# LSH attention and a gated FFN on one core: five of a head's sixteen coefficient blocks from DMA transposes instead of comparisons

## The chip, the core and the metric

The kernel runs on one core of one Trainium2 chip. The metric is the device time of one execution in microseconds (us), the median of several runs. The profile comes from one further execution.

## What is computed

The input x is 16 batches (B) of 512 tokens (S) of 128 features. The attention has 16 heads (H) of 8 features. Each token gets one bucket per head, from the signs of six projections of its query, and the score of two tokens is multiplied by 63 if their buckets agree and by 62 if not. Cut to what matters:

```python
proj = jnp.einsum('bshe,en->bshn', qa, hyperplanes)
buckets = jnp.einsum('bshn,n->bsh', (proj >= 0).astype(jnp.int32), 2 ** jnp.arange(6))
scores = jnp.einsum('bhsd,bhtd->bhst', q, q) / jnp.sqrt(jnp.float32(E))
same = (b_hs[:, :, :, None] == b_hs[:, :, None, :]).astype(scores.dtype)
attn = jax.nn.softmax(scores * (NB - 2 + same), axis=-1)
out = jnp.einsum('bhst,bhtd->bhsd', attn, v)
```

Before and after the attention there are layer norms and a residual; then comes a feed-forward network (silu gate of two products, two gelu layers of 512 x 512, one product back to 128), again with layer norms and a residual. The matrix `same` of a head is symmetric: block (i, t) of 128 x 128 tokens is the transpose of block (t, i).

## The kernel before

One head j is 512 x 512 coefficients, in four row tiles t of 128 query tokens (NT = 4). The work of a head passes through the engines like this:

- **SP** (the sync engine's DMA queue, taken strictly in turn) gathers the head's operands: `ql` and `qr`, the query in three bf16 parts (lines 798 and 812), and `bb`, the head's 512 buckets in bf16, repeated on all 128 partitions (line 825).
- **PE** makes the scores `sp` of a row tile in a PSUM bank (line 847), one matmul each.
- **DVE** makes the coefficients `co` of a row tile (line 865): it compares the 512 buckets of `bb` with the bucket of the query token on each partition (`bj`, a pointer scalar) and adds 62. Then DVE multiplies `co` with `sp` into the f32 tile `l` and takes the maximum of each row in the same instruction (line 894).
- After two heads, a small DVE transpose (923), a DMA to memory (`md`, 928) and a DMA back that repeats the maxima over the partitions (`mb`, 940) bring the row maxima into the layout that is needed; **POOL** subtracts `mb` from `l` (947), **ACT** takes the exponential (952).
- When four heads are done, PE multiplies with the values (`av`, 973), which frees the four `l` buffers. Then follow the division, the residual and layer norm, and the feed-forward network of the batch (lines 1041 to 1188), which runs beside the heads of later batches.

The buckets of a batch are written to memory as `bkd` in rows: BR = 3 rows of BC = 172 values at a pitch of BP = 174. So `bb` has 522 columns, of which a comparison reads 3 x 172 = 516; `co` is one run of 516 per row tile, and the last four aren't used.

The order of all instructions is written down ahead of time by a small planner (class `Order`, lines 47 to 187). Every step is a process that asks for buffers, waits for events and offers an instruction to an engine with an estimated cost and a rank; the engine takes the offered instruction of the lowest rank (comparisons have 4, the logits of line 894 have 5, so a comparison that is ready goes first). Each engine then runs its list in that order. DMAs are modelled as one queue with a rate (DMA_RATE, KB per us, 160 before) and a landing time of 2.6 us. The planner's costs set the order only, not what an instruction takes on the chip.

Buffers around the change: 11 tiles `l` of 8 KB per partition (LB), four sets of `ql`, `qr` and `bb` (`row_bufs`), four `co` tiles of one row tile each (`co_bufs`), three PSUM banks for `sp`. A `co` buffer is given back after its own row tile's logits, and a set of rows after the head's last.

Of the kernel before, what the change touches and what calls it, by code (L numbers as in the profile page):

```python
# [21 lines left out]
P = 128  # L22
# [24 lines left out]
class Order:  # L47
# [7 lines left out]
    LAT = 0.3  # L55
    OWN = 0.2
    DMA_LAT = 2.6
    DMA_RATE = 160.0
    SWITCH = 4.0
    TABLE = 1.28  # L60

# [129 lines left out]
def tile_lsh_attention_ffn(  # L191
# [31 lines left out]
    DA = DH + 1  # L223
    NP = 3
    KS = NP * NP * DH
    BR, BC, BP = 3, 172, 174
    ROOT = float(np.float32(E**-0.5))
    GROUPS = (1, 2, 6, B)
    LATE = 20
# [2 lines left out]
    SCALE = 1.0 / math.sqrt(E)  # L232
    AHEAD = 1
    MH = 2
    LB = 11
    SLOTS = H * NT
    N = B * SLOTS

# [86 lines left out]
        mxpads.append(mp)  # L325
    bkts = []
    for i in range(2):
        bk = const.tile([H, BR, BP], BF16, name=f"bkt{i}")
        nc.vector.memset(bk, 0.0)
        bkts.append(bk)  # L330

# [6 lines left out]
    def dve(cost, rank, emit):  # L338
        return ("op", "DVE", cost, emit, rank, None)

    def act(cost, rank, emit, table=None):
        return ("op", "ACT", cost, emit, rank, table)
# [4 lines left out]
    def dma(kb, rank, emit, held=True, cost=0.35):  # L347
        return ("dma", "SP", cost, emit, rank, None, kb, held)

    def get(kind):  # L350
        return ("get", kind)
# [4 lines left out]
    def events(n):  # L356
        return [Event() for _ in range(n)]
# [4 lines left out]
    banks = Pool("b", 2)  # L362
    logit_bufs = Pool("l", LB)
    row_bufs = Pool("r", 4)
    co_bufs = Pool("co", 4)
    mx_bufs = Pool("mx", 2)
    mb_bufs = Pool("mb", 3)
    h_bufs = Pool("h", 3)
# [213 lines left out]
    def prep(b):  # L582
# [59 lines left out]
        def buckets():  # L642
            yield wait(read)
            kp = yield get(banks)
            pp = bank(kp, f"pp_{b}")
            yield pe(
                0.86,
                2,
                lambda: nc.tensor.matmul(
                    pp[0 : H * NH, :],  # L650
                    lhsT=hp_sb.rearrange("e h n -> e (h n)"),
                    rhs=qs,
                    start=True,
                    stop=True,
                ),
            )
            bits = p1.tile([H * NH, S], BF16, tag="bits", name=f"bits_{b}")
            yield dve(
                0.66,
                1,  # L660
                lambda: nc.vector.tensor_scalar(
                    bits, pp[0 : H * NH, :], hb_sb, 0.0, op0=ALU.add, op1=ALU.is_ge
                ),
            )
            od.put(banks, kp)
            kp = yield get(banks)
            bkp = bank(kp, f"bkp_{b}")
            yield pe(
                0.3,
                2,  # L670
                lambda: nc.tensor.matmul(bkp[0:H, :], lhsT=pw, rhs=bits, start=True, stop=True),
            )
            bk = bkts[b % 2]

            def evict():
                nc.scalar.copy(
                    bk[:, 0 : BR - 1, 0:BC],
                    bkp[0:H, 0 : (BR - 1) * BC].rearrange("h (r c) -> h r c", c=BC),
                )
                nc.scalar.copy(  # L680
                    bk[:, BR - 1, 0 : S - (BR - 1) * BC], bkp[0:H, (BR - 1) * BC : S]
                )

            yield act(0.53, -2, evict)
            od.put(banks, kp)
            bkd = dram.tile([H, BR * BP], BF16, tag="bkd", name=f"bkd_{b}")

            def write():
                yield dma(
                    16,  # L690
                    0,
                    lambda: nc.sync.dma_start(out=bkd, in_=bk.rearrange("h r c -> h (r c)")),
                )
                bkds[b] = bkd
                od.set(wrote)

            od.spawn(write())
            kp = yield get(banks)
            bjp = bank(kp, f"bjp_{b}")

            def columns():
                for t in range(NT):
                    nc.tensor.matmul(
                        bjp[:, ts(t, H)],
                        lhsT=bits[:, ts(t, P)],
                        rhs=pw,
                        start=True,
                        stop=True,
                    )

            yield pe(0.4, 2, columns)
            bj = p2.tile([P, NT * H], F32, tag="bj", name=f"bj_{b}")
            yield dve(0.13, 1, lambda: nc.vector.tensor_copy(bj, bjp[:, 0 : NT * H]))
            bjs[b] = bj
            od.put(banks, kp)
            od.set(columned)
# [70 lines left out]
    def gather(j, tag):  # L787
        b, h = divmod(j, H)
        yield wait(prepared[b])
        ql = p1.tile([KS, S], BF16, tag=f"ql{tag}", name=f"ql_{j}")  # L790
        qr = p1.tile([KS, S], BF16, tag=f"qr{tag}", name=f"qr_{j}")
        bb = p1.tile([P, BR * BP], BF16, tag=f"bb{tag}", name=f"bb_{j}")
        rows[j] = (ql, qr, bb, tag)

        yield dma(
            74,
            1 + j * 1e-3,
            lambda: nc.sync.dma_start(
                out=ql,
                in_=qds[b][1][h]  # L800
                .rearrange("i d s -> (i d) s")
                .unsqueeze(1)
                .to_broadcast([NP * DH, NP, S]),
            ),
            held=False,
            cost=0.75,
        )
        queue = nc.sync if j else nc.scalar
        yield dma(
            74,  # L810
            1 + j * 1e-3,
            lambda: queue.dma_start(
                out=qr,
                in_=qds[b][0][h]
                .rearrange("d j s -> (d j) s")
                .unsqueeze(0)
                .to_broadcast([NP, NP * DH, S]),
            ),
            held=False,
            cost=0.72 if j else 0.05,  # L820
        )
        yield dma(
            132,
            1 + j * 1e-3,
            lambda: nc.sync.dma_start(out=bb, in_=bkds[b][h].partition_broadcast(P)),
            cost=0.43,
        )
        od.set(gathered[j])
# [9 lines left out]
    def scores():  # L838
        for j in range(B * H):
            yield wait(gathered[j])  # L840
            ql, qr = rows[j][0:2]
            for t in range(NT):
# [9 lines left out]
                sps[j * NT + t] = (sp, k)  # L852
                od.set(scored[j * NT + t])

    def coeffs():
        for j in range(B * H):
            b, h = divmod(j, H)
            yield wait(gathered[j])
            bb = rows[j][2]
            for t in range(NT):  # L860
                k = yield get(co_bufs)
                co = p1.tile([P, BR * BC], BF16, tag=k, name=f"co_{j}_{t}")

                def emit(c=t * H + h, bb=bb, co=co, b=b):
                    nc.vector.tensor_scalar(  # L865
                        co,
                        bb.rearrange("p (r c) -> p r c", c=BP)[:, :, 0:BC],
                        bjs[b][:, c : c + 1],
                        float(NBKT - 2),
                        op0=ALU.is_equal,  # L870
                        op1=ALU.add,
                    )

                yield dve(0.39, 4, emit)
                cos[j * NT + t] = (co, k)
                od.set(weighed[j * NT + t])
                od.loose()

    def logits():
        for j in range(B * H):  # L880
            kl = yield get(logit_bufs)
            if j < SINGLES or j % MH == 0:
                km, pair = (yield get(mx_bufs)), []
                mx = mxpads[int(km[2:])]
            l = p1.tile([P, NT, S], F32, tag=kl, name=f"l_{j}")
            base = len(pair) * NT
            for t in range(NT):
                i = j * NT + t
                yield wait(scored[i])
                yield wait(weighed[i])  # L890
                (sp, ks), (co, kc) = sps.pop(i), cos.pop(i)

                def emit(t=t + base, sp=sp, co=co, l=l[:, t, :], mx=mx):
                    nc.vector.tensor_tensor_reduce(  # L894
                        out=l,
                        in0=co[:, 0:S],
                        in1=sp,
                        scale=1.0,
                        scalar=-3.0e38,
                        op0=ALU.mult,  # L900
                        op1=ALU.max,
                        accum_out=mx[:, t : t + 1],
                    )

                yield dve(0.61, 5, emit)
                od.put(score_banks, ks)
                od.put(co_bufs, kc)
                if t < NT - 1:
                    od.loose()
            od.put(row_bufs, rows.pop(j)[3])  # L910
            ls[j] = (l, kl)
            pair.append((j, l))
            if j < SINGLES or len(pair) == MH:
                od.spawn(maxima(pair, mx, km))
            if j % GH == GH - 1:
                od.spawn(attend(j // GH))
            od.loose()
# [403 lines left out]
```

## Time and profile before

| what | value |
|---|---|
| median of 3 runs | 1372.26 us (1371.28 to 1372.66) |
| the profiled execution, its own time | 1373.08 us |
| the profiled execution, its span | 1371.3 us |
| mean granted TensorE clock | 0.991 |
| busy over the span: PE, DVE, ACT, POOL | 96%, 90%, 82%, 89% |
| DMA: moved, mean rate | 175.39 MB, 128 GB/s |
| L865 comparison, 1024 times | 455.0 us busy, 472 ns each |
| L894 logits, 1024 times | 665.7 us busy, 681 ns each |
| L947 subtraction on POOL, 256 times | 1156.1 us busy, 4552 ns each |

How to read it: "busy" counts the time in which an engine has at least one instruction under way; the records of PE overlap each other, so a busy PE isn't one at its limit. A line such as "L865 DVE TENSOR_SCALAR co<-bb,bj" is the group of instructions that line 865 of the kernel issues on DVE, writing `co` from `bb` and `bj`; after the bar stand its busy time in us, the mean of one in ns, and how long the engine had been idle before these instructions and what ended that idle time. The DMAs that SP issues are shown with the time SP takes to issue them, not the time until the data lands.

### The profile page before, as it was taken

To read this page: it belongs to the slowest core of one execution; us is meant where nothing else is said; L and a number is where in the kernel's file an instruction comes from. 1 tells how busy PE (TensorE), PEld (TensorE's weight loads), DVE (VectorE), ACT (ScalarE), POOL (GpSimd) and SP (SyncE) were. 2 spreads that over 40 slices of the span, in tenths; PEclk is the share of its full clock that TensorE was granted. 3 is DMA by queue.
4 is the path that set the end of the run, shared out by engine and by line. 5 is a ranking of instruction groups with operands and counts; after the bars stand their busy time and mean duration, and the time that the engine had idled before them with its cause. 6 is when DMAs were issued, how large, how long until landed. Compare 5 with 4: busy or idle time off the path is not lost.

```text
span 1371.3 us, 21177 instructions
## 1 busy us (share of the span) xinstructions
PE 1317.3 (96%) x5922; PEld 550.9 (40%) x5922; DVE 1236.0 (90%) x3989; ACT 1127.8 (82%) x1607; POOL 1217.1 (89%) x319
## 2 busy tenths in 40 slices
PE   9999999999889999999999999999999999999996
PEld 3433334334334434343434434343434434343443
DVE  5999999999889999999999999999999999998210
ACT  2567798999779888988989888988989888988852
POOL 1599999999999999999999999999999999999400
PEclk9999999999899999999999999999999999999998
DMA  5756455445435455445545455454545454453000
GB/s 143 194 148 157 133 150 145 140 140 141 134 106 153 125 130 142 138 138 132 147 116 147 129 134 135 139 139 135 142 124 141 135 134 135 132 122 101 24 8 8
DMA packets 159837, 175.39 MB, mean 128 GB/s; under 512 B 34280, under 2 KB 117480, under 8 KB 159720
## 3 DMA queue, kind: packets, MB, share of 16 engines
q1 hardware_dynamic: 156909, 170.56, 45.4%
q10 hardware_dynamic: 2811, 3.48, 0.8%
q8 instruction: 47, 0.77, 0.2%
q14 instruction: 70, 0.57, 0.1%
HBM read 154.81 MB, written 19.17 MB: 127 GB/s over the span
## 4 chain that ended last, share of the span: by engine, by line
PE 50%; DVE 24%; POOL 9%; issue 8%; DMA 6%; ACT 2%; SPq 1%; POOLq 0%; DVEq 0%; ACTq 0%
PE hp L1122 18%; PE av L973 12%; DVE l L894 11%; PE sp L847 9%; DVE co L865 8%; POOL l L947 8%; PE w L1088 4%; PE yp L1156 3%; DMA mb<-md 3%; DMA bb<-bkd 1%; DMA qd<-q 1%; PE op L994 1%; PE vp L760 1%; POOL rs_x L561 1%; DMA qr<-qd 1%
## 5 line engine op out<-in xcount | busy, mean ns | idle before, releaser
L947 POOL TENSOR_TENSOR l<-l,mb 128x2048 f32<-128x2048 f32 x256 | 1156.1, 4552 | 43.4 <-DVE mxpad L894 24.0
L894 DVE CUSTOM_DVE_ANT_0 l<-co,sp 128x512 f32<-128x512 bf16 x1024 | 665.7, 681 | 13.8 <-PE av L973 6.9
L952 ACT ACTIVATE l<-l 128x2048 f32<-128x2048 f32 x256 | 484.6, 1907 | 40.9 <-POOL l L947 39.4
L1122 PE MATMUL hp<-h,h 128*128 128x512 f32 x1024 | 498.6, 596 | 0.3 <-ACT h L1135 0.3
L865 DVE TENSOR_SCALAR co<-bb,bj 128x516 bf16<-128x516 bf16 x1024 | 455.0, 472 | 3.3 <-DMA bb<-bkd 3.1
L847 PE MATMUL sp<-qr,ql 72*128 72x512 bf16 x1024 | 358.0, 382 | 26.7 <-DVE mxpad L894 22.5
L1122 PEld LDWEIGHTS hp<-h,h 128*128 128x128 f32 x1024 | 190.1, 190 | 185.6 <-issue 151.6
L973 PE MATMUL av<-l,vaug 128*32 128x512 f32 x2048 | 263.6, 603 | 0.0
L847 PEld LDWEIGHTS <-ql 72*128 72x128 bf16 x1024 | 94.1, 97 | 313.9 <-issue 290.7
L1088 PE MATMUL w<-xnt_f,w 128*128 128x512 f32 x256 | 132.0, 601 | 2.5 <-ACT a L1074 2.4
L952 ACT ACT_TABLE_LOAD x86 | 110.3, 1283 | 1.5
L1251 PE MATMUL activity<-still 128*128 128x512 bf16 x402 | 106.6, 385 | 1.0 <-DVE still L280 1.0
L973 PEld LDWEIGHTS av<-l,vaug 128*32 128x32 f32 x2048 | 47.4, 109 | 116.5 <-issue 93.9
L894 DVE DVE_READ_ACCUMULATOR2_ANT mxpad<- 128x1 f32 x1024 | 85.7, 84 | 0.0
L450 POOL TENSOR_TENSOR rs_y<-ve_y,mhalf 128x4 f32<-128x4 f32 x16 | 16.1, 1006 | 67.1 <-issue 34.7
L1057 DVE TENSOR_TENSOR h<-w,a 128x512 f32<-128x512 f32 x64 | 43.7, 682 | 35.2 <-PE w L1088 30.3
L1135 ACT ACT_TABLE_LOAD x58 | 74.4, 1283 | 0.9
L987 ACT COPY avs<-av 128x512 f32<-128x512 f32 x64 | 37.0, 578 | 40.0 <-PE av L973 39.9
L1088 PEld LDWEIGHTS w<-xnt_f,w 128*128 128x128 f32 x256 | 46.9, 191 | 53.1 <-issue 21.8
L1156 PEld LDWEIGHTS yp<-w,h 128*128 128x128 f32 x512 | 65.0, 196 | 7.3 <-issue 4.0
L1156 PE MATMUL yp<-w,h 128*128 128x128 f32 x512 | 66.6, 281 | 0.1
L1251 PEld LDWEIGHTS <-still 128*128 128x128 bf16 x402 | 39.1, 99 | 56.5 <-issue 19.0
(94 smaller groups left out, 941.7 us busy)
## 6 DMA issues: line engine op xcount, KB each, us to landing
mb<-md SPq DMA_DIRECT2D x256, 256.0 KB
bb<-bkd SPq DMA_DIRECT2D x256, 130.5 KB
ql<-qd SPq DMA_DIRECT2D x256, 72.0 KB
qr<-qd SPq DMA_DIRECT2D x255, 72.0 KB
qd<-q SPq DMA_DIRECT2D x96, 128.0 KB
xta<-in_L_attn_x_dram SPq DMA_DIRECT2D x16, 256.0 KB
xtr<-in_L_attn_x_dram SPq DMA_DIRECT2D x16, 256.0 KB
out_dram<-y SPq DMA_DIRECT2D x16, 256.0 KB
```

The source lines that it names most:

```text
L847: nc.tensor.matmul(sp, lhsT=ql[:, ts(t, P)], rhs=qr, start=True, stop=True)
L865: nc.vector.tensor_scalar(co, bb.rearrange("p (r c) -> p r c", c=BP)[:, :, 0:BC], bjs[b][:, c : c + 1], float(NBKT - 2), op0=ALU.is_equal, ...
L894: nc.vector.tensor_tensor_reduce(out=l, in0=co[:, 0:S], in1=sp, scale=1.0, scalar=-3.0e38, op0=ALU.mult, op1=ALU.max, accum_out=mx[:, t : ...
L947: lambda: nc.gpsimd.tensor_tensor(l, l, mb.unsqueeze(1).to_broadcast([P, NT, S]), op=ALU.subtract),
L952: yield act(1.82, 0, lambda: nc.scalar.activation(l, l, AF.Exp, scale=SCALE), "exp")
L973: nc.tensor.matmul(av[k * Q : (k + 1) * Q, :], lhsT=va[:, t, c : c + Q], rhs=ls[gg * GH + k][0][:, t, :], start=(t == 0), stop=(t == NT - 1),)
L1057: lambda: nc.vector.tensor_tensor(h[:, c, :], g2, a, op=ALU.mult),
L1088: lambda: nc.tensor.matmul(gp, lhsT=w_sb[which][:, 0, ts(c, P)], rhs=xnt, start=True, stop=True),
L1122: lambda i=i: nc.tensor.matmul(hp, lhsT=w[:, i, ts(c, P)], rhs=hin[:, i, :], start=(i == 0), stop=(i == NC - 1),),
L1135: nc.scalar.activation(h[:, c, :], hp, AF.Gelu, scale=sc[:, c : c + 1])
L1156: nc.tensor.matmul(yp[:, ts(t, E)], lhsT=h[:, i, ts(t, P)], rhs=w_sb["w3"][:, i, :], start=(i == 0), stop=(i == NC - 1),)
L1251: nc.tensor.matmul(bk, lhsT=still, rhs=still.unsqueeze(1).to_broadcast([P, NT, P]), start=start, stop=stop,)
```

## The change

Row tiles 0 and 1 make part of the coefficients of the later row tiles (TURNED = 2). Row tile 0 is compared in full, 4 blocks of 128 columns. Row tile 1 is compared in its blocks 1 to 3 only, row tiles 2 and 3 in blocks 2 and 3 only. The missing five blocks (1,0), (2,0), (3,0), (2,1) and (3,1) come from two DMA transposes per head, which SP issues: one turns the blocks 1 to 3 of row tile 0, the other the blocks 2 and 3 of row tile 1. The logits of row tile t wait for the transposes that write into it (none for 0, one for 1, two for 2 and 3).

For this, `co` becomes one tile of a whole head (4 x 512 bf16, 4 KB per partition), with three buffers, given back after the head's last logits. The buckets are kept in 4 rows of 128 at a pitch of 130, so that a comparison reads 4, 3, 2 or 2 rows of 128 columns. The `l` buffers go from 11 to 10. The planner is told a DMA rate of 240, a cost of 0.6 us for a transpose on SP, and new costs of the comparisons.

```diff
-    DMA_RATE = 160.0
+    DMA_RATE = 240.0
...
-    BR, BC, BP = 3, 172, 174
+    BP = P + 2
+    TURNED = 2
...
-    LB = 11
+    LB = 10
...
-    co_bufs = Pool("co", 4)
+    co_bufs = Pool("co", 3)
...
+    turns = [events(TURNED) for _ in range(B * H)]
+
+    def turn(j, co, i):
+        yield dma(
+            2 * 32 * (NT - 1 - i),
+            0.5,
+            lambda: nc.sync.dma_start_transpose(
+                out=co[:, i + 1 :, ts(i, P)], in_=co[:, i, (i + 1) * P :]
+            ),
+            cost=0.6,
+        )
+        od.set(turns[j][i])
+
     def coeffs():
...
-            bb = rows[j][2]
+            bb = rows[j][2].rearrange("p (r c) -> p r c", c=BP)
+            k = yield get(co_bufs)
+            co = p1.tile([P, NT, S], BF16, tag=k, name=f"co_{j}")
+            cos[j] = (co, k)
             for t in range(NT):
-                k = yield get(co_bufs)
-                co = p1.tile([P, BR * BC], BF16, tag=k, name=f"co_{j}_{t}")
-
-                def emit(c=t * H + h, bb=bb, co=co, b=b):
+                r = min(t, TURNED)
+
+                def emit():
+                    c = t * H + h
                     nc.vector.tensor_scalar(
-                        co,
-                        bb.rearrange("p (r c) -> p r c", c=BP)[:, :, 0:BC],
+                        co[:, t, r * P :].rearrange("p (r c) -> p r c", c=P),
+                        bb[:, r:, 0:P],
                         bjs[b][:, c : c + 1],
                         float(NBKT - 2),
                         op0=ALU.is_equal,
                         op1=ALU.add,
                     )
 
-                yield dve(0.39, 4, emit)
-                cos[j * NT + t] = (co, k)
+                yield dve(0.08 + 0.09 * (NT - r), 4, emit)
                 od.set(weighed[j * NT + t])
-                od.loose()
+                if t < TURNED:
+                    od.spawn(turn(j, co, t))
+            od.loose()
...
                 yield wait(weighed[i])
-                (sp, ks), (co, kc) = sps.pop(i), cos.pop(i)
+                for e in turns[j][:t]:
+                    yield wait(e)
+                sp, ks = sps.pop(i)
+                co = cos[j][0][:, t, :]
...
-                        in0=co[:, 0:S],
+                        in0=co,
...
-                od.put(co_bufs, kc)
                 if t < NT - 1:
                     od.loose()
+            od.put(co_bufs, cos.pop(j)[1])
             od.put(row_bufs, rows.pop(j)[3])
```

The eviction of the buckets on ACT becomes one copy in place of two, and the `bkt`, `bkd` and `bb` tiles take the new shape.

More of the change, by code (lines that the diff above doesn't have):

```diff
@@ L327, in tile_lsh_attention_ffn @@
     for i in range(2):
-        bk = const.tile([H, BR, BP], BF16, name=f"bkt{i}")
+        bk = const.tile([H, NT, BP], BF16, name=f"bkt{i}")
         nc.vector.memset(bk, 0.0)
@@ L676, in evict @@
                 nc.scalar.copy(
-                    bk[:, 0 : BR - 1, 0:BC],
-                    bkp[0:H, 0 : (BR - 1) * BC].rearrange("h (r c) -> h r c", c=BC),
-                )
[L680 to L684, printed above, removed]
+                    bk[:, :, 0:P], bkp[0:H, :].rearrange("h (r c) -> h r c", c=P)
+                )
+            yield act(0.5, -2, evict)
             od.put(banks, kp)
-            bkd = dram.tile([H, BR * BP], BF16, tag="bkd", name=f"bkd_{b}")
+            bkd = dram.tile([H, NT * BP], BF16, tag="bkd", name=f"bkd_{b}")
             def write():
@@ L791, in gather @@
         qr = p1.tile([KS, S], BF16, tag=f"qr{tag}", name=f"qr_{j}")
-        bb = p1.tile([P, BR * BP], BF16, tag=f"bb{tag}", name=f"bb_{j}")
+        bb = p1.tile([P, NT * BP], BF16, tag=f"bb{tag}", name=f"bb_{j}")
         rows[j] = (ql, qr, bb, tag)
```

## The prediction

> **What bounds the kernel now.** I read the table of stretches first, because shares over the whole span mix start, steady part and tail. Columns: length, then busy time (and instructions) of PE, PE weight loads, DVE, ACT and POOL, then granted clock, DMA share and GB/s.
>
> ```profile
> 754.20:831.30 77.10, 74.97 (x342) 31.75 (x342) 76.61 (x250) 67.40 (x86) 74.72 (x20) 1.00 0.49 136
> 831.30:908.40 77.10, 76.14 (x350) 31.55 (x348) 76.52 (x246) 69.50 (x88) 76.09 (x20) 1.00 0.50 136
> ```
>
> The chain of work repeats every two batches (the same yp step at 596, 750 and 904 us), so a batch of 16 heads takes 77.1 us, a head 4.82 us. The span of 1371.3 us is 256 x 4.82 = 1234 us and 137 us of start and tail. In a steady batch DVE is busy 76.5 us (99%), POOL 74.7 to 76.1 us. Three engines are full together; a cheaper one hands the end to the next.
>
> Second, the groups of instructions by shape, for the prices:
>
> ```profile
> L947 POOL TENSOR_TENSOR l<-l,mb 128x2048 f32<-128x2048 f32 x256 | 1156.1, 4552 | 43.4 <-DVE mxpad L894 24.0 <-DMA mb<-md 14.1 <-ACT junk L407 3.1
> ...
> L894 DVE CUSTOM_DVE_ANT_0 l<-co,sp 128x512 f32<-128x512 bf16 x1024 | 665.7, 681 | 13.8 <-PE av L973 6.9 <-PE sp L847 5.1
> L865 DVE TENSOR_SCALAR co<-bb,bj 128x516 bf16<-128x516 bf16 x1024 | 455.0, 472 | 3.3 <-DMA bb<-bkd 3.1
> ...
> L661 DVE TENSOR_SCALAR bits<-pp,hb_sb 96x512 bf16<-96x512 f32 x16 | 11.8, 737 | 0.0
> ...
> L455 DVE TENSOR_SCALAR nm_f<-mv_f,rs_f 128x1 f32<-128x1 f32 x64 | 9.2, 208 | 3.8 <-POOL rs_f L450 3.8
> ```
>
> DVE almost never waits. POOL needs 16 x 4.552 + 3 x 1.006 = 75.9 us per batch, 98% of the period. PE's busy time overlaps itself; by starts (0.43 us for an f32 record of hp or w, 0.215 sp, 1.85 per 16 av) its batch needs about 73 us.
>
> Third, SP, whose instructions are not counted as busy: its own waits (total us, times, longest) and its timeline.
>
> ```profile
> SPq L928 <- DVE co L865: 227.2, 104, 6.0
> SPq L798 <- PE sp L847: 134.4, 146, 3.3
> ...
> SPq L940 <- POOL l L947: 46.7, 50, 5.0
> ```
> ```profile
> 718.00 0.55 SPq L928 DMA_DIRECT2D md<-mt  x1
> 718.60 0.72 SPq L812 DMA_DIRECT2D qr<-qd  x1
> 719.38 0.43 SPq L825 DMA_DIRECT2D bb<-bkd  x1
> 720.37 0.77 SPq L798 DMA_DIRECT2D ql<-qd  x1
> 721.25 0.45 SPq L940 DMA_DIRECT2D mb<-md  x1
> ```
>
> SP takes its DMAs strictly in turn. A head needs ql 0.78 + qr 0.72 + bb 0.41 + mb 0.40 + half of md 0.56 = 2.59 us, its share of the batch's twelve others (qd, xta, xtr, out, bkd, at 0.33 to 0.6) about 0.28, and some 0.08 us between neighbours (718.60 to 719.38 for a 0.72), about 0.35: 3.2 of 4.82 us. So 1.6 us per head are free, and SP already stands behind DVE for long stretches.
>
> **The change, part by part.** *Comparisons (L865).* L661 and L455 give a TENSOR_SCALAR's fixed time: 737 - 512/0.96 = 204 ns, and 208 for one element. L865 then is 204 + 516/(2 x 0.96) = 473 ns, as measured: two elements per cycle. A head had 4 x 516 = 2064 elements and keeps 512 + 384 + 256 + 256 = 1408. At the same rate that takes 656/1.92 = 342 ns off 4.82 us of DVE, 87 us over the span.
>
> *The form of the comparison, a rule against the change.* Source rows go from 3 of 172 to 4, 3, 2 and 2 of 128. The row before: 2 elements per cycle.[...] By the row the comparisons cost 16 x 0.342 = 5.5 us less per batch[...]. At worst one comparison stops DVE for nearly a whole POOL instruction each head, with only one l (0.6 us) done beside it: 4.6 + 4.1 - 0.7 = 8.0 us, 2185 us. I keep the row's rate for the likeliest case, and the rule as a rival.
>
> *Transposes on SP.* Added: two per head, 512 in all. No row shows one. Nearest rows for issuing: md 0.56, ql 0.78 (the longest, with the most row pieces). At 0.56 with gaps, 1.3 us fit in the free 1.6; at 0.78, 1.7 us, SP needs 4.9 us per head and is full. A full queue that also waits on DVE and POOL in turn cannot run at 100%; at 95% that is 5.16 us per head. Not below nothing: issuing is added work. I take 0.78 at 95%: 256 x (5.16 - 4.82) = +87 us, less nothing for DVE, which is no longer last.
>
> *Transposes on the DMA engines.* 5 x 32 KB = 160 KB per head beside 175.39 MB / 256 = 685 KB. As plain traffic the share goes from 0.49 to 0.60: hidden.[...] No row decides; I take little extra[...].
>
> *The new waits.* Each transpose waits on SP for its comparison; behind it stand md and mb, for which POOL waits, and the gathers. On DVE, l of t = 1 waits for one transpose and t = 2, 3 for two, with all DVE work behind. md to the mb that reads it takes 2.8 us in the timeline (709.44 to 712.28), the nearest row for a landing. With three co buffers of a whole head, comparisons may lead by one to two heads, 4.8 to 9.6 us: cost nothing, if that lead is real; without it up to 2.8 us per head. I take nothing, since SP's lateness is already counted.
>
> *Eleven to ten l buffers.* DVE waited for av to free l 6 times, 6.9 us in all: between nothing and one such wait (up to 2.3 us) in each of 64 groups, 147 us; I take 5 us. The reason it can't gain: a buffer less adds only waits.
>
> *The rest at nothing:* one ACT copy in place of two (0.43 + 0.28 to about 0.57 us, 16 times, ACT is 88% busy), 520 for 522 columns of bb. The planner's rate of 240 moves emission order, not work.
>
> **Sum.** 1371.3 + 87 + 5 = 1463 on the profiled span; its own execution is 1373.1, 1.8 longer than its span, and the median 1372.3 lies 0.8 under that. About 40 heads of the start and the end run while SP has room; there DVE's 0.34 us per head is a gain, 13 us off: **1450 us**.
>
> **Rivals.**
> - *Shared ports*[...]: 1570 to 2185 us, middle near 1800. For: the row counts become even, POOL is busy 97% of the time[...]. Against:[...] the instruction's encoded shape is not in the profile.
> - *It works, on the other side:* transposes land inside the lead, issue near md's 0.56, and DVE falls to 4.43 us per head. Then POOL's 75.9 us per batch ends last: at most 1.2 x 16 = 20 us. It still waits for ve and mb now and then (2 us per batch now), so I give two thirds: 1358 us, 1352 to 1369. It decides as long as a transpose's issue stays under 0.7 us (SP's free 1.6 us halved, less the gap). For: DVE is at 99%. Against: POOL at 98% and PE at 95% leave little.
> - *Nothing to see:* same as that, with the lost l buffer eating it: 1370 to 1375.
>
> **Chances.** SP or DMA queue full 0.36[...]; shared ports 0.33; works 0.25; nothing to see 0.06. A difference under 0.2% can't be told from none here. Faster 0.25, same 0.06, slower 0.69. The range from 1352 to 1850 leaves out the upper half of the shared-port case (0.17) and a sliver below.[...]
>
> **What would show it.** DVE busy down by 80 to 90 us with TENSOR_SCALAR near 471, 404 and 337 ns: the comparison step. Records of 337, 304 and 271 ns, gaps on DVE or POOL of 1 to 4 us beside them, or POOL instructions well over 4.55 us: shared ports. SP issue of a transpose near 0.8 us, SP without gaps, and POOL waiting for mb: my likeliest.[...] POOL over 99% in steady batches: the gain. I am wrong if the issue is near 0.5 us[...].

## The result, and the profile after

| | before | after |
|---|---|---|
| median | 1371.77 us (4 runs) | 2171.43 us (2154.74 to 2192.97, 4 runs) |
| ratio | | 1.579, 95% interval 1.568 to 1.590 |
| span of the profiled execution | 1371.3 us | 2177.5 us |

The ratio leaves out the execution of 2192.97 us, which ran at a lower granted clock (0.820) than the other three (0.831 to 0.834).

The change makes the kernel 58% slower. The forecast was 1450 us, and the time lies outside its range too (1352 to 1850). A head now takes (2177.5 - 137)/256 = 7.97 us in place of 4.82: close to the 8.0 us, 2185 us, that the prediction had priced for the worst case of a rival, "shared ports".

From the page after, its head and the chain of work that ended last:

```profile
span 2177.5 us, 22144 instructions
## 1 busy us (share of the span) xinstructions
PE 1575.4 (72%) x5901; PEld 627.8 (29%) x5901; DVE 1881.4 (86%) x3989; ACT 1135.4 (52%) x1593; POOL 1217.1 (56%) x319
...
DVE 48%; PE 25%; issue 15%; DMA 8%; SPq 3%; ACT 1%; POOL 0%; DVEq 0%; POOLq 0%; ACTq 0%
```

POOL works exactly as long as before (1217.1 us) in a span 806 us longer; it is now idle 44% of the time. DVE, which was to get lighter by 87 us, is busy 645 us longer. The groups of DVE by shape say where:

```profile
L880 DVE TENSOR_SCALAR co<-bb,bj 128x256 bf16<-128x256 bf16 x512 | 713.2, 1400 | 0.0
L913 DVE CUSTOM_DVE_ANT_0 l<-co,sp 128x512 f32<-128x512 bf16 x1024 | 677.6, 676 | 101.3 <-PE sp L844 47.9 <-PE av L992 42.1 <-DMA co<-co 9.2
L880 DVE TENSOR_SCALAR co<-bb,bj 128x512 bf16<-128x512 bf16 x256 | 297.5, 1162 | 48.8 <-DMA bb<-bkd 48.6
L880 DVE TENSOR_SCALAR co<-bb,bj 128x384 bf16<-128x384 bf16 x256 | 102.6, 401 | 0.0
```

The comparison of 256 columns takes 1400 ns on average, that of 384 columns 401 ns. The longer one is faster. Its source has three rows, that of the others four or two. 401 ns is near 204 + 384/1.92 = 404, the old rate: 1.92 columns per ns, about twice what the rows L661 and L455 of the kernel before show, (737 - 208)/511 = 1.04 ns a column. The logits (676 ns) are as before. DVE waits for a transpose's landing only 9.2 us in all.

The same tile's view, with minimum, median and maximum in ns, shows that the mean hides two kinds of record, and what SP pays for a transpose:

```profile
L880 DVE TENSOR_SCALAR co<-bb,bj x1024: 239/352/4685, 26.4 to 2070.5; 128x512 bf16<-128x512 bf16 x86, 128x256 bf16<-128x256 bf16 x85
...
L860 SPq DMA_TRANSPOSE co<-co x512: 1167/1205/2642, 27.5 to 2074.6; - x171
```

A comparison can be as short as 239 ns and as long as 4685 ns, a little over one POOL instruction (4528 ns). By the trace, 235 of the 768 comparisons with four or two rows take over 0.6 us, and every one of them ends within 0.08 to 0.16 us after a POOL instruction has ended. None of the other 533 lies wholly inside a subtraction of POOL (L966). Of the 256 with three rows the longest takes 418 ns; 55 of them lie wholly inside a subtraction, at 401 ns in the mean.

Who waits on SP, and POOL's wait for the maxima (us in total, times, longest):

```profile
SPq L860 <- DVE co L880: 430.7, 165, 9.6
```
```profile
POOL l L966 <- DMA mb<-md: 544.0, 92, 29.0
```

SP takes its DMAs in turn: by the trace, none of its 1846 issues here begins before the one ahead of it has ended. It isn't full in this kernel: from 900 to 1000 us its issues take 65% of the time and the short gaps between them, some 0.09 us each, 6%; for the rest it waits, most of all for comparisons. POOL's wait for `mb`, which the prediction named as a sign of a full SP, stands here beside an SP with room.

### The profile page after: what moved, and what is told of

Same layout as the page of the kernel before. It is cut to its first block, busy times and chain, and to the rows that moved or that the text cites. A ratio compares the mean times of both kernels' runs of the same rounds, so it can differ in the third digit from the quotient of the medians.

```text
span 2177.5 us, 22144 instructions
## 1 busy us (share of the span) xinstructions
PE 1575.4 (72%) x5901; PEld 627.8 (29%) x5901; DVE 1881.4 (86%) x3989; ACT 1135.4 (52%) x1593; POOL 1217.1 (56%) x319
## 4 chain that ended last, share of the span: by engine, by line
DVE 48%; PE 25%; issue 15%; DMA 8%; SPq 3%; ACT 1%; POOL 0%; DVEq 0%; POOLq 0%; ACTq 0%
DVE co L880 30%; DVE l L913 14%; PE hp L1141 8%; PE av L992 6%; PE sp L844 6%; DMA bb<-bkd 4%; DMA co<-co 2%; PE w L1107 2%; DVE h L1076 1%; PE activity L1270 1%; SPq L860 1%; DMA ql<-qd 1%; PE yp L1175 1%; DVE mxpad L913 1%; PE op L1013 1%
## 5 line engine op out<-in xcount | busy, mean ns | idle before, releaser
L966 POOL TENSOR_TENSOR l<-l,mb 128x2048 f32<-128x2048 f32 x256 | 1154.8, 4528 | 738.4 <-DMA mb<-md 544.0
L880 DVE TENSOR_SCALAR co<-bb,bj 128x256 bf16<-128x256 bf16 (+2 forms) x1024 | 1101.9, 1091 | 48.8 <-DMA bb<-bkd 48.6
L844 PE MATMUL sp<-qr,ql 72*128 72x512 bf16 x1024 | 429.3, 444 | 560.0 <-DVE mxpad L913 554.8
L913 DVE CUSTOM_DVE_ANT_0 l<-co,sp 128x512 f32<-128x512 bf16 x1024 | 677.6, 676 | 101.3 <-PE sp L844 47.9
L1141 PE MATMUL hp<-h,h 128*128 128x512 f32 x1024 | 577.2, 675 | 0.0
L1141 PEld LDWEIGHTS hp<-h,h 128*128 128x128 f32 x1024 | 216.9, 216 | 435.4 <-issue 411.1
L992 PE MATMUL av<-l,vaug 128*32 128x512 f32 x2048 | 297.8, 685 | 2.1 <-DVE y L1199 2.1
L844 PEld LDWEIGHTS <-ql 72*128 72x128 bf16 x1024 | 105.6, 107 | 488.5 <-issue 461.6
L1107 PE MATMUL w<-xnt_f,w 128*128 128x512 f32 x256 | 158.8, 721 | 7.9 <-DVE h L1076 7.2
L1154 ACT ACTIVATE h<-hp,h2s 128x512 f32<-128x512 f32 x64 | 41.8, 685 | 53.9 <-PE hp L1141 53.5
L474 ACT ACTIVATE yb<-o,nm_o,rs_o 128x128 f32<-128x128 f32 x64 | 29.5, 461 | 74.9 <-DVE nm_o L456 65.7
```

Source lines behind the costliest of these rows:

```text
L844: nc.tensor.matmul(sp, lhsT=ql[:, ts(t, P)], rhs=qr, start=True, stop=True)
L880: nc.vector.tensor_scalar(co[:, t, r * P :].rearrange("p (r c) -> p r c", c=P), bb[:, r:, 0:P], bjs[b][:, c : c + 1], float(NBKT - 2), op0 ...
L913: nc.vector.tensor_tensor_reduce(out=l, in0=co, in1=sp, scale=1.0, scalar=-3.0e38, op0=ALU.mult, op1=ALU.max, accum_out=mx[:, t : t + 1],)
L966: lambda: nc.gpsimd.tensor_tensor(l, l, mb.unsqueeze(1).to_broadcast([P, NT, S]), op=ALU.subtract),
L992: nc.tensor.matmul(av[k * Q : (k + 1) * Q, :], lhsT=va[:, t, c : c + Q], rhs=ls[gg * GH + k][0][:, t, :], start=(t == 0), stop=(t == NT - 1),)
L1107: lambda: nc.tensor.matmul(gp, lhsT=w_sb[which][:, 0, ts(c, P)], rhs=xnt, start=True, stop=True),
```

## The experiments

The theory after the result, "shared ports": a comparison with an even number of source rows (here four or two) can't run while POOL's subtraction runs. The name stands for a reason that no run here shows; the runs show the wait alone. Rivals: "SP and DMA" (the transposes' issue or traffic sets the pace), "late transposes" (DVE waits for their landing), and the tenth `l` buffer.

**Even rows alone, on the kernel before.** No transposes, eleven `l` buffers.

```diff
-    BR, BC, BP = 3, 172, 174
+    BR, BC, BP = 4, 128, 130
```

> The kernel before with one edit: the buckets in four rows of 128 (pitch 130) in place of three of 172. No transposes, eleven l buffers. Theory 'shared ports'[...]: comparison records with a minimum near 337 ns, a mean over 1000 ns, longest near 4.7 us; DVE per head 4.82 - 1.89 + 1.00 = 3.9 us, plus POOL's 4.6, less 0.7 done beside it: 7.8 us per head, 137 + 256 x 7.8 = about 2130 us. Rival 'SP and DMA' (the 1.2 us that SP spends on each transpose set the pace): 1372 us within 5. Rival 'late transposes' (DVE waits for their landing): 1372 us.

Measured: 2259.68 us, ratio 1.647 (1.644 to 1.651). One line of shapes, with no transpose in the kernel, makes it slower than the whole change does. The comparisons (minimum, median and maximum), then one stretch of the timeline (start, length, engine, instruction):

```profile
L865 DVE TENSOR_SCALAR co<-bb,bj x1024: 300/345/4714, 26.2 to 2143.7; 128x512 bf16<-128x512 bf16 x171
```
```profile
998.94 18.10 POOL L947 TENSOR_TENSOR l<-l,mb 128x2048 f32<-128x2048 f32 x4
...
999.86 3.76 DVE L865 TENSOR_SCALAR co<-bb,bj 128x512 bf16<-128x512 bf16 x1
...
1005.24 7.43 DVE L865 TENSOR_SCALAR co<-bb,bj 128x512 bf16<-128x512 bf16 x2
...
1013.80 3.39 DVE L865 TENSOR_SCALAR co<-bb,bj 128x512 bf16<-128x512 bf16 x1
```

POOL's four instructions follow each other at 4.525 us, so they end at 1003.46, 1007.99, 1012.51 and 1017.04. DVE's comparisons end at 1003.62, 1012.67 (the second of two) and 1017.19: each time 0.15 us after a POOL instruction ends, wherever it began. In the whole trace 250 comparisons take over 0.6 us, and every one ends 0.146 to 0.158 us after a POOL instruction. So a comparison waits until the POOL instruction that is under way is over, and two comparisons in a row wait for two of them. The 0.15 us look like the comparison's own work: in the changed kernel it is again 0.15 us for 512 columns and 0.08 us for 256, and with the short subtraction below 256 columns more take 70 ns, so these would be 0.14 and 0.07 us (an estimate from 351 and 281 ns). Both rivals gave 1372 us for this kernel, so neither can be the cause of this loss.

The time is 130 us above the 2130 that was expected. From 400 to 1000 us DVE is busy 561.4 of 600 us, 94% of (2254.8 - 137)/256 = 8.27 us per head, which is 7.7 us, near the 7.8 of the sum; the sum left out the other 6%, in which DVE is idle.

**Odd rows, with everything else of the change.** Buckets in 33 rows of 16 at a pitch of 17, the last row empty.

```diff
-    BP = P + 2
+    BC = 16
+    BR = S // BC + 1
+    BP = BC + 1
...
-            co = p1.tile([P, NT, S], BF16, tag=k, name=f"co_{j}")
+            co = p1.tile([P, NT, S + BC], BF16, tag=k, name=f"co_{j}")
...
-                        co[:, t, r * P :].rearrange("p (r c) -> p r c", c=P),
-                        bb[:, r:, 0:P],
+                        co[:, t, r * P :],
+                        bb[:, r * (P // BC) :, 0:BC],
```

(To make room, the scale of w3 is loaded through an `l` buffer at the start, as that of w2 is.)

> The changed kernel with the comparisons in odd row counts: buckets in 33 rows of 16 at a pitch of 17, the last row empty, so that the comparisons read 33, 25, 17 and 17 rows and write one run each; co rows 528 long. Transposes, ten l buffers and all waits stay. Theory 'shared ports': no comparison waits; records 204 ns + columns/1.92 = 479, 412, 346 and 346 ns; POOL or SP sets the pace, SP with 3.2 + 2 x 1.28 = 5.8 us per head: about 1610 us. Rival 'SP and DMA' as the cause of all: stays within 5% of 2171 us. Rival 'late transposes': stays there too, with DVE idle before l.

Measured: 1723.68 us, ratio 1.257 (1.253 to 1.260). So the row counts, odd in place of even, are worth 448 us of the 800 here. DVE's groups of this kernel:

```profile
L915 DVE CUSTOM_DVE_ANT_0 l<-co,sp 128x512 f32<-128x512 bf16 x1024 | 679.3, 678 | 103.7 <-DMA co<-co 49.0 <-PE sp L846 24.3 <-PE av L994 23.4
L882 DVE TENSOR_SCALAR co<-bb,bj 128x272 bf16<-128x272 bf16 x512 | 177.8, 354 | 0.0
L882 DVE TENSOR_SCALAR co<-bb,bj 128x528 bf16<-128x528 bf16 x256 | 128.5, 502 | 310.1 <-DMA bb<-bkd 309.0
L882 DVE TENSOR_SCALAR co<-bb,bj 128x400 bf16<-128x400 bf16 x256 | 108.7, 425 | 0.0
```

354, 502 and 425 ns against the 346, 479 and 412 expected; no comparison in this kernel takes longer than 507 ns. Comparisons cost 415 us in all in place of 1113. But the kernel is still 351 us slower than before, and 114 us above the 1610 that was expected. DVE now stands idle 309 us for the gather of `bb`, whose issue on SP comes late, and 49 us for transposes that have not landed. SP's own rows in one stretch:

```profile
920.25 2.50 SPq L862 DMA_TRANSPOSE co<-co  x2
922.81 0.74 SPq L811 DMA_DIRECT2D qr<-qd  x1
923.59 0.44 SPq L824 DMA_DIRECT2D bb<-bkd  x1
924.15 0.36 SPq L961 DMA_DIRECT2D mb<-md  x1
924.60 1.21 SPq L862 DMA_TRANSPOSE co<-co  x1
```

The rows follow each other within 0.1 us. From 1000 to 1080 us SP's issues take 90% of the time and the short gaps between them 9%, so the queue is full; in a batch of the kernel before (700 to 777 us) they take 62% and 6%. The second cause is SP's queue.

**Ten `l` buffers alone, on the kernel before.**

```diff
-    LB = 11
+    LB = 10
```

> The kernel before with ten l buffers in place of eleven and nothing else. All theories: a side matter, 1372 to 1385 us. If it alone costs more than 20 us, the tenth buffer is a cause of its own.

Measured: 1436.51 us, ratio 1.048 (1.046 to 1.050): 64 us, over the threshold that was set. The logits of DVE and POOL's wait for the maxima in this kernel:

```profile
L894 DVE CUSTOM_DVE_ANT_0 l<-co,sp 128x512 f32<-128x512 bf16 x1024 | 663.6, 680 | 64.6 <-PE av L973 59.1 <-PE sp L847 4.5
```
```profile
POOL l L947 <- DMA mb<-md: 82.8, 24, 19.6
```

DVE waits 59.1 us for `av` to free a buffer (6.9 before), and POOL 82.8 us for the maxima (14.1 before), presumably because DVE hands them over later.

**The transposes alone, unread.** The comparisons of the kernel before (all sixteen blocks, three rows), ten `l` and six `co` buffers, the planner's rate of 240, and two transposes per head into a scratch tile.

```diff
+            lambda: nc.sync.dma_start_transpose(
+                out=scr[:, 0:n, :], in_=co[:, (i + 1) * P : S]
+            ),
```

> The kernel before (three rows of 172, all sixteen blocks compared, ten l buffers, six co buffers, planner's DMA rate 240) plus the two transposes of each head from row tiles 0 and 1 into a scratch tile that nobody reads, so DVE never waits for one. Theory 'shared ports': this is only the price of SP's queue, an added 2 x 1.28 us per head on SP's 3.2: if SP then is last, 137 + 256 x 5.8 = about 1610 us; never near 2171. Rival 'SP and DMA': most of the 800 us, 2000 us or more.

Measured: 1719.16 us, ratio 1.253 (1.251 to 1.256). DVE's comparisons:

```profile
L882 DVE TENSOR_SCALAR co<-bb,bj 128x516 bf16<-128x516 bf16 x1024 | 463.5, 473 | 287.3 <-DMA bb<-bkd 190.6 <-DMA sc<-co 93.5 <-DVE mxpad L920 0.3
```

From 900 to 980 us SP's issues take 90% of the time and the short gaps 9%: as in the odd-row kernel, the queue is full. The 1610 us that were expected of both are missed because a head takes 6.2 us of SP, (1715.8 - 137)/256, and not 5.8. Most of that lies in the issues, which add up to 0.9 x 6.17 = 5.55 us per head where 2.59 + 0.28 + 2 x 1.2 = 5.27 were assumed: a transpose takes 1.25 us in the mean (1.21 in the median), and the gather of `bb` 0.47 us in place of 0.42. With ten buffers as the step below it, 512 transposes cost 283 us although nobody waits for their data: DVE waits 190.6 us for `bb`, which SP issues late, and 93.5 us for `co` buffers that a transpose still reads.

**The same, one block per transpose.** Two blocks per head in place of five, the same 512 instructions.

```diff
-                out=scr[:, 0:n, :], in_=co[:, (i + 1) * P : S]
+                out=scr[:, 0:1, :], in_=co[:, (i + 1) * P : (i + 2) * P]
```

> The kernel with the two unread transposes per head, each cut to one block of 128 x 128 (two blocks per head in place of five; the same 512 transposes). If SP's issue sets the pace and its 1.2 us don't depend on the number of blocks: 1719 us within 2%. If it does depend on them (about 0.4 us a block): 3.2 + 2 x 0.6 = 4.4 us per head, 1440 to 1480 us. If the DMA engines' work sets the pace: in between or lower, with SP idle.

Measured: 1692.32 us, 27 us less than with five blocks. SP's price of the instruction:

```profile
L860 SPq DMA_TRANSPOSE sc<-co x512: 1093/1136/3027, 28.0 to 1584.1; - x171
```

1136 ns for one block against a median of 1205 for two or three: about 1.1 us is fixed, and a block adds some 46 ns. The means differ by 55 ns (1192 against 1247), and 512 x 55 ns = 28 us is the whole gain. It is the number of instructions on SP that counts, and hardly the data.

**One transpose per head, odd rows.** As the odd-row kernel, with TURNED = 1: three blocks of sixteen by one transpose.

```diff
-    TURNED = 2
+    TURNED = 1
```

> The changed kernel with odd row counts and one transpose per head in place of two (row tiles 1 to 3 compare blocks 1 to 3; three of sixteen blocks come by DMA). SP needs 3.2 + 1.28 = 4.5 us of a head: if SP's queue is all that is left of the loss beside the tenth l buffer, about 1436 us (that buffer's price alone) to 1480 us, with SP's issues near 85 to 90% of the time. If the loss comes from DVE waiting for the transposes' landing instead: over 1550 us.

Measured: 1475.05 us, ratio 1.073 (1.070 to 1.077); SP's issues take 83% of the time from 800 to 880 us and the short gaps 8%. Taking one of the two transposes away returns 249 us, and what is left lies 39 us above the price of the tenth buffer alone. So SP's queue and the buffer explain most of what the wait for POOL doesn't; the 39 us are not explained, though DVE still waits 77 us for `bb` here.

**A short subtraction on POOL.** The other side of the wait: the comparisons keep their even rows, and POOL's instruction leaves out 504 of every 512 columns.

```diff
-                l, l, mb.unsqueeze(1).to_broadcast([P, NT, S]), op=ALU.subtract
+                l[:, :, 0:8], l[:, :, 0:8], mb[:, 0:8].unsqueeze(1).to_broadcast([P, NT, 8]), op=ALU.subtract
...
-        yield act(1.82, 0, lambda: nc.scalar.activation(l, l, AF.Exp, scale=SCALE), "exp")
+        yield act(1.82, 0, lambda: nc.scalar.activation(l, l, AF.Exp, scale=SCALE * 1e-3), "exp")
```

> The changed kernel with POOL's subtraction cut to 8 of each row tile's 512 columns (the rest of the maxima isn't subtracted; the exponent is scaled by a further 1/1000 so that nothing overflows). All else stays, even rows and transposes too. Theory 'shared ports': with POOL's instruction far under 1 us the even-row comparisons go back to their own length, 337 and 271 ns (four elements per cycle on top of 204 ns), none over 1.5 us, and SP's queue is what is left: about 1700 us, as with odd rows. If the even-row comparison is slow by itself: mean stays over 1000 ns and the time near 2171 us.

Measured: 1718.03 us, ratio 1.252 (1.247 to 1.256). DVE's groups:

```profile
L880 DVE TENSOR_SCALAR co<-bb,bj 128x256 bf16<-128x256 bf16 x512 | 140.1, 281 | 0.0
L880 DVE TENSOR_SCALAR co<-bb,bj 128x384 bf16<-128x384 bf16 x256 | 103.5, 404 | 0.0
L880 DVE TENSOR_SCALAR co<-bb,bj 128x512 bf16<-128x512 bf16 x256 | 89.9, 351 | 353.8 <-DMA bb<-bkd 353.0
```

The same instructions that took 1400 and 1162 ns take 281 and 351 beside a POOL instruction of 255 ns: 70 ns more for 256 more columns, where the old rate would take 133. The longest comparison of all takes 417 ns. The three-row form stays at 404, the old rate. So an even-row comparison isn't slow by itself; in the changed kernel 512 x (1400 - 281) + 256 x (1162 - 351) = 781 us of DVE's busy time are waits for POOL. The time is again about 1720 us, as in the other kernels in which SP is full.

**The subtraction in four instructions.** The whole work, in pieces of one row tile.

```diff
-            lambda: nc.gpsimd.tensor_tensor(
-                l, l, mb.unsqueeze(1).to_broadcast([P, NT, S]), op=ALU.subtract
-            ),
+            lambda: [
+                nc.gpsimd.tensor_tensor(l[:, t, :], l[:, t, :], mb, op=ALU.subtract)
+                for t in range(NT)
+            ],
```

> The changed kernel with POOL's subtraction as four instructions of one row tile (about 1.15 us each) in place of one of 4.53 us. Theory 'shared ports, held for a whole instruction': the longest comparison falls from 4.69 us to about 1.15 + 0.34 = 1.5 us, and since a stop is shorter and less of DVE's other work is lost, the time falls too, to 1750 to 2000 us.[...]

Measured: 1738.22 us, ratio 1.266 (1.262 to 1.271), just under the range that was expected. POOL's pieces, and the longest comparison:

```profile
L967 POOL TENSOR_TENSOR l<-l,mb 128x512 f32<-128x512 f32 x1024 | 1273.3, 1280 | 304.4 <-DMA mb<-md 228.2 <-DVE co L880 31.5 <-DVE mxpad L913 24.6
```
```profile
L880 DVE TENSOR_SCALAR co<-bb,bj x1024: 238/410/1516, 25.4 to 1631.3; 128x512 bf16<-128x512 bf16 x86, 128x256 bf16<-128x256 bf16 x85
```

From 4685 to 1516 ns, as forecast: a comparison waits for one POOL instruction, be it 4.5 or 1.28 us long. Had it waited for POOL's work as a whole, shorter instructions would not have shortened its longest wait. By the means of the even-row comparisons (686 and 795 ns, against 281 and 351 with the short subtraction) 321 us of waits are left in DVE's busy time, but DVE has room for them: from 900 to 980 us SP's queue is as full as in the odd-row kernel, and the time is within 1% of that kernel's.

**Twelve `l` buffers, on the kernel before**, with two `h` buffers of the feed-forward network in place of three; and that second edit alone.

```diff
-    LB = 11
+    LB = 12
...
-    h_bufs = Pool("h", 3)
+    h_bufs = Pool("h", 2)
```

> The kernel before with twelve l buffers; the 8 KB come from the feed-forward network's h buffers, two in place of three. The tenth buffer's loss (64 us from eleven to ten) suggests that POOL and DVE live on that lead: if it goes on, 1340 to 1365 us, faster than both kernels. If eleven is already enough, or the network runs late with two h buffers: 1372 us or more.

> The kernel before with two h buffers in place of three and eleven l buffers: the price of the memory that the twelfth l buffer takes. 1372 to 1400 us; the difference to the kernel with twelve l buffers is that buffer's own effect.

Measured: 1372.55 us, ratio 0.999 (0.998 to 1.000), and 1380.83 us for the two `h` buffers alone, ratio 1.006 (1.004 to 1.008). The twelfth buffer gives about 8 us and the memory for it costs as much. The step from eleven to ten is eight times the one from twelve to eleven. Neither of the two kernels is faster than the kernel before.

## Why the prediction was wrong

- **What bounds the kernel** (DVE, POOL and PE full together): right for the kernel before. It fits that even rows alone (+887 us), ten buffers alone (+64) and the transposes on top of ten buffers (+283) each cost time: none had slack to disappear in.
- **The form of the comparison** is the step that failed: "I keep the row's rate for the likeliest case, and the rule as a rival." The row of 472 ns was measured on three source rows, the very form that the change gives up, so it was no evidence for four and two rows. In place of 342 ns saved, the comparisons of a head gained 781/256 = 3.1 us of waiting for POOL, with 235 long waits in 256 heads. The even-row kernel and the short and split subtractions show it from both sides. The longest comparison goes with POOL's instruction: 4685 ns beside 4528, 1516 beside 1280. No row of the kernel before showed the "rule" that the prediction kept as a rival.
- **The rival's price** of 8.0 us per head, 2185 us, is within 1% of the measured 2171, and in part by luck. It was 4.1 us of DVE's own work (4.82 less 0.34 and a further 0.37, for all comparisons at twice the old rate, which no row of the kernel before showed) and 3.9 us behind POOL, with DVE never idle. Measured from 400 to 1000 us, DVE is busy 90% of 7.97 us, 7.2 us: the 4.1, and 3.1 of waiting. The other 0.8 us are idle time, which the price left out; any cost of the transposes and of the lost buffer lies in it too.
- **The three-row comparison** was priced by that rival at twice the old rate too (304 ns). It ran at the old one (401 to 404 ns) and never waited: 418 ns at the longest. The forms with 17, 25 and 33 rows did neither as well (507 ns at the longest). Why an odd count differs is not shown.
- **The comparisons' saving** of 342 ns per head was computed rightly for the old rate, and was larger still where POOL was out of the way (4 x 472 = 1888 ns per head against 351 + 404 + 2 x 281 = 1317 ns with the short subtraction). It bought nothing: in that kernel and in the odd-row one SP is last, not DVE.
- **Transposes on SP**: the mechanism was right, the size wrong. The term was 0.78 us, from `ql`; a transpose takes 1.2 us. "At 95%", the author's estimate, was a little low: with its gaps counted, the queue is 98 to 99% full in the kernels that SP bounds. With 1.2 us for the issue and gaps of 0.09, the prediction's own sum gives (3.2 + 2.6)/0.95 = 6.1 us per head, near the 6.2 of the unread transposes. The forecast of +87 us for this term stands against +283 us of the transposes alone. A new kind of instruction was priced by the longest of another kind, and SP's free 1.6 us were overdrawn by 1 us, not by 0.1.
- **Transposes on the DMA engines**: rightly taken as little. Five blocks in place of two cost 27 us, and these are SP's longer issues. Were it the blocks that set the pace, three fewer of five would have saved far more of the 283 us.
- **The new waits on DVE**: taken at nothing, and small in the changed kernel (9.2 us), where DVE is late itself. In the odd-row kernel, where it isn't, DVE waits 49 us for landings, so the comparisons' lead doesn't hide all of it.
- **Eleven to ten buffers**: taken at 5 us, measured 64, inside its two bounds (nothing to 147). The wait for `av` was small before because eleven buffers about suffice: a twelfth gives 8 us, the eleventh 64.
- **The rival that it works** was wrong by its own condition, issue under 0.7 us: a transpose takes 1.2.

The three causes don't add up in any order. Even rows alone cost 887 us on the kernel before, but only 448 us on top of the other two. It fits that DVE then waits in time in which SP would have been late anyway: its idle time before `bb` is 309 us in the odd-row kernel and 48.6 in the changed one. The chain ten buffers (+64), transposes (+283), removal of comparisons (+5), even rows (+448) leads to the measured 2171, but each amount is that of its place. The transposes-only kernel has six `co` buffers and a planner's rate of 240 as well, so the 283 include what these do, and how much that is stays open.

## What to carry to other kernels

Before a shape is changed, ask at what rate the old shape ran, and beside what: a duration is a price only for the shape it was measured on. POOL's work filled 98% of a steady batch before, so comparisons that wait for POOL could not keep out of its way, and 0.35 us of work could wait for up to 4.5 us of another engine's. Splitting the long instruction or taking an odd row count each cured it here (the longest comparison fell to 1516 and 507 ns). Price a new DMA by its issue on the queue that must take it, count what is free there, and look for the buffer that pays for the memory.

## What was not expected of the hardware

- POOL doesn't pay: in the even-row kernel four of its instructions follow at 4.525 us while comparisons slip in at the ends, and its mean in the changed kernel is 4528 ns against 4552 before. The prediction's lower price (1570 us), which added the comparisons' time to POOL's, was not seen in any run. Short pieces take longer in all (4 x 1280 = 5120 ns), but not because of the comparisons: a piece beside which no even-row comparison runs takes 1273 ns, the others 1281.
- A DMA transpose takes SP about 1.1 us plus 46 ns a block, 1.5 times the longest of the plain DMAs here.
- The TensorE clock granted fell from 0.991 to 0.832 in the changed kernel, whose PE is busy 72% in place of 96%, and an f32 record of `hp` went from 596 to 675 ns. How much of the loss this makes stays open: PE holds 25% of the chain that ended last, 544 us, and at 596/675 of their length these would be some 64 us shorter (an estimate). It goes with the other losses: with less lost, the clock is higher (0.92 in the odd-row kernel, 0.98 with ten buffers).
